# A cross-attention and ternary FFN kernel on one core: the context in one transfer, a silu of a constant column, a new instruction order

## The chip, the cores and the metric

The kernel runs on one core of a Trainium2 chip. The metric is the device time of one execution in microseconds (us), as the median of several runs. A core has a matmul engine (PE, with its weight loads shown apart as PEld), VectorE (DVE), ScalarE (ACT), GpSimd (POOL), and SyncE (SP), which here issues every transfer. Each engine works through its own instructions in program order; semaphores join them. Sixteen DMA engines carry out the transfers.

## The reference

For each of 8 batches there are 512 tokens of 512 features (x) and a context of 64 memory tokens of 512 features, with a mask. Cut to what matters:

```python
def linear_bit(x, w, g):                       # 8-bit activations, ternary weights
    x = g * x * rsqrt(mean(x*x) + 1e-8)
    s = 127 / clip(max|x|, 1e-4); xq = clip(round(x*s), -128, 127) / s
    m = mean|w|;  wq = round(tanh(w / (m + 1e-8))) * arctanh(m)
    return xq @ wq.T

n = layernorm(x)
a = softmax(where(mask, n @ ctx.T / sqrt(512), -1e30))
x = x + a @ ctx                                # zero where a batch's mask is all false
n = layernorm(x)
h = silu(linear_bit(n, w1, g1)) * linear_bit(n, w2, g2)    # 512 -> 2048
x = x + linear_bit(h, w3, g3)                  # 2048 -> 512
```

Each of w1, w2, w3 holds 2048 x 512 numbers in f32, 4 MB. The mean of |w| has to be known before a weight can be made ternary, so a whole weight passes through the chip before its first matmul.

## The kernel before, in words

**Tiles.** A batch is four tiles of 128 tokens, 32 tiles in all. For a tile, the work is a chain: layer norm and the scores (`pre`: statistics L560, the scaled tile `t` and its f16 parts `xh` L582 to 592, their transposes `xT`, the score matmuls `psc` L602, the masked scores `sc` L614 to 624), the exponentials (`expo`, L645, ScalarE), the softmax's scaling and the readout (`post`, L659 to 691: `ph`, its transpose `pT`, the matmuls `po` L683 from `ms`), the rms norm and 8-bit rounding of the FFN's input (`quantise_x`, L721 to 800: `xm`, the gain on POOL L736, the row maximum L741, the rounded `xm` L799/800, its transpose `zT`), the gate and up matmuls (L883, 16 groups of 8 matmuls per batch for each weight), silu (`gate`, L899, ScalarE), the product (L927, VectorE), its square (L932), the gain g3 (L940, POOL or VectorE), the maximum (L964), rounding (L997/999), a DMA transpose of the result (`hT`, L1002), and the down projection (`pd`, L825), which runs `LAG` = 3 tiles behind the gate.

**Weights.** Each weight comes in four pieces of 1 MB (`raw`, `load_w`). `measure_w` sums |w| of each piece on ScalarE (L353) or VectorE (L357) and joins the sums by a small matmul (`pm`, L363); `quantise_w` makes the pieces ternary (`tq`: tanh's threshold as a scaled rounding, L386 on POOL or VectorE, L387 on ScalarE), transposes them on PE (L396) and clips them into `w1T`, `w2T`, `w3T` (L390). The raw pieces, x of each batch and other large tiles share 9 buffers.

**The context.** `load_x(b)` loads, for an even batch, the contexts of two batches into one tile `both` (128 x 512, 256 KB, L473), from which `measure_mem` gets their scale; and for each batch the tile `mem`, which holds the same 64 rows twice, in partitions 0 to 63 and 64 to 127. It comes by two transfers of 128 KB (L478). `split_mem` makes two f16 parts of it (`ms`: the rounded part by L533 on ScalarE, the rest by L536 on VectorE), and transposes them to `mT` for the scores. `mem` has two buffers, `both` one.

**What sets the order.** The program first records every operation with its engine, a planner's cost in ns, what it reads and writes, and sometimes other engines that could do it. A planner that isn't part of the kernel has chosen an order and an engine for each; the result is the text `ORDER` (L151 to 190), decoded in `Plan.order`. Buffers are handed out in that order, and each engine gets its instructions in it. So the costs in the listing have no effect at run time, other than through the `ORDER` that was made with them. All loads, stores and DMA transposes are issued on SP's one queue, in that order. Before the change SP's order at the start is: mask, both_0, first half of mem_0, half of x_0, second half of mem_0, half of x_0, the four pieces of w1, g1, w2's first three pieces (two of them into space that w3T will take), g2, w2's last, x_1, both halves of mem_1, two pieces of w3, both_2, a piece, g3, x_2, the last piece, mem_2, both_4, the transpose mT_1, x_3, mem_3, and then the first transposes xT_1.

Of the kernel before, what the change touches and what calls it, by code (L numbers as in the profile page):

```python
# [41 lines left out]
AF = mybir.ActivationFunctionType  # L42
# [3 lines left out]
P = 128  # L46
# [13 lines left out]
PE, DVE, ACT, POOL, DMA = "PE", "DVE", "ACT", "POOL", "DMA"  # L60
DVE2 = "DVE2"
# [87 lines left out]


ORDER = """  # L151
c-jTQedKy+q5$yo@|^eQob#M>o^#G~UY3@Y?~m_~mM$$_y0o;kv@~?-($LV*(9*qHS{k~vG&D4{S3{SEhW==1XlUqOEnONKS{fQ!8d_R
f`lF@cem)c>QkVi1q!1OQa#WtmQU!`oMe2nrQ4#8uDpMg<p<+~=s!|CmNu{VXm7(g?h3-;Ux=r<{4%MJ;G^9VFn$&>8^oJCphZLbl)KB
QIs2bI$BlOqQXH=A4QFnSkPpCEZhMrOz>R;$BHKS(ikp3k-r{2;TdPnW47@egL)RZ03-%}GdPUq+oHKxy0p8h*^p%V0+dQewtLMQ1TsV
V)Wzo3^a#XxpWQ*?p;mIh3b7MT(a8N>j3L1RXw-=p{Roc*3AOvpr-1O0nuNmu9$^C!AWpXey_!mMb-PPqkprr%*Ubed_<Ev7~{=~pJkZ
0Ri1qA~lR+jN|%(;Yg&beSYW*c4M>a!i{E*)DzLip+}b(F-QR9=Ir51R3xy^M>s(HRc0m!@S4TnI7}X_L&$vWJ};b**!O4TA;z?K^#n&
&zKqaCG$R00DopWU?}$3-?42lWV&F)WWk#4vtKhgFl7ep$Kb$p_&!)MBQ^ozY>OX&HS-12VaM#JV8b@qEz@PMpv||~5m<vUn1LO$Wko^
aCZG(COj`I0GY1J42|qA@W0LF!U?Ihh#2x#0Ce3DqP|vVX$g(t>74FQF*@7IK6CTW-&9i_lu<r;vP-HL6ci_NEY>7RxW%k5Y*n%(xXZF
HY*(10}PjF=mTv0fI8(U-VY@L0uG4Nz7;2rJ^y22a&p8@13um?9#1!e9eA+E>)`2z0Xw*Ye~PzM99!oB4l0Dv?&aaB$PPbtPNK%A>_ge
wV45OPB<#X%6^5QuVft}HY_f;)3>xSmiEk{kv^Xo6pHRiVUPI09CH;#yo^7zrWBa#yL!i*f`2uFV~U92W%(?#k7<SN<rxfF<_|R$PbsB  # L160
}egRsliclL|=0UzQzxPE%$p)<N^O8oP-#^6}#LUdBeTRJ09{+zR!&XN<jQXXbL?J2zx#zr}-Oa^E>X&J(N(0^J_6KKe&z9<wHKhzo=^=
%lG&sAK~Xhf`4*Rekj)ksOI<-KjQLyLn!haf$&42z>m3=^eRq;_xKWj;?v?n_#I#8D`JK3^Plofe!_LcwKU>q!XNpiu#sv)34P8d<drb
yqvH2`SBwZV{wy@a8$ac5%8Qtk@5)p7nxFGnEs1~Q-wG*t!T(HH^G$T;FG5@dVp-hqq7s$P{FZ<4P#MVyk&-AeE{S4HxbR8wA&zAzUIi
jH#gsUa3sPK&sX3`7hT=_#t9RiS!c%-zcOp^$A^Z;?5!+}iHlz=Qw(ufVq;G_s&=J~VUTR86-3v)!DZNTn=_noLln|2+;#`V}C;292#J
!jok78Dwi0`N;aVi$XAH<nxh#gcxTdANH#f4;xWz<4dloQYLT`H<j-bqNgihmW~RjVSBKS%$k?xlxx7i;1ag>p@*i#HKSJuxEN(nr!vh
SCg0Wl`#jL>h=UIU)7rP(l)x=VDD>iVJZi-sOy(lp<0~p2~HpE;r=0e34U9T1v}TIG0y)QNqfvq>}WI`_hL}TPjPhN>(CrSzX9ixg&*2
Oxdaf={t!iznAAqMCnOcxuWLesM1ina#dX@Z8-{uQd7yxDWxFil(aID{#(i@9i=aK<gz@Kwn|r7$}?#o$F(M`$O&zyY~+?wmACR(+AD9
AfzpCE*oOt>Tlo%qN?tiAOXVqNbV^C<M`ZwCAW(Afr0mqVvX>J|Q7$U4@Tu%oQ7b8Z<y|=st4awbmG_i{`o8jO1;CnekSTbANv*E56{v
l#i116)hC>Cykz&B9V#6`?;7mEg2b{pH{+SZO3q;xzifRP@#Guqr<<ylDQKRZcIjC#ptfaK08iz4BR8ug8x>gz{;8jVf8TF!+VMZINSv
3QbFsDw{u^KUE))3aziB*B2mW5bLs|DD%(pnWpv<0leqgq$z*3|k4)?o)`wGo`c9=xhE*i@rhPMgDmwm?O=REc&{=h|0lRXeLoxPoJ?0  # L170
axnhYC|t-6Rn}H;Z5DZnYz&S@T9fWwR(UL?V_HwwmMgP>Jiqoi~iK^YF?{reU;M3`a^AMPnFVMwSoE#>{;K!7j0nuL7i&9)7n~7k7+<(
YfCMvU$lw7(^pzYn`wKitmX8LCh9NxN9tC4)puGJMGdI$^@85gUW~og(%;oO#zBjtiZ<1OwnSI`sLl1fo<LpgW38yCQ4OuoK>If%hYnT
-mGp!DiT0iz(`Wk8s-uTK)ZW*t`c-@CBdv=*GHzPWC>eGAu61;zxAh(x=rz5suTc`+^sY|yzJc`{%A<u2QNyg8OTDM}Q4!V5ve7_yv_Y
ThuLd%PsAAl8${6W2V}w?E+8CpOvC-?spY)-D(EuIwlO8hwI_o2YLIotEszFfPc%YOqb+&rK*rFY37zn9G(wG`!BWs4}N3=&X<AC0vjd
MnEb7kzDxr2>Y^f1;&!rU1f<ELor#L&;s-pQGw`80rWMa0OPWAlQbd9pG_28+hTpiE>goTr&JW=_tSm`(G0ls7&!n#RE(=2r$~wT*9#q
&YYC#?CC5cV}rFjlZCi@q_VK1DHkgYV6H|fh}y7%!3)4cOzmpEMmQwM>C6W#@ULRB`dVr=Bqh1TV~8mSUKD=KQ`lf*F2e@m<c_pr}VNF
v4Ax&o7T{}SShP&rOc5zvcAM2zFH5bgVScxD&mZp#}S;h($@c)bF*d*&4u-axiL$4ZPu-f)x~GCY%Z<5wJ@XB*4*HgRj^*H9$uOYe6xy
H%PQcDSv4zG*ID8|zM4;`V<qv;Y+Ds`Y^^Y~?xtvMth@Ca>lGtwh__b7{kipO?W_;no>RtA9JgxtVXmzz9^t+-z`wv-JjRs!u%h<U+Tj
WYZrpycpP0fDe!&2%7~vEy*$ErthF!K}IE@KD;HG`EYwi)Z>^QFD(3!Y<+`vh@iCcJWPw~*6;I<9yh%>{l_Qp=zqI<%3dyUUH?xbw!?%
gXE?Hj)1ihaQer(^#E*WIz*#!H8?M>eu!Hnyj3%X!D{+65ch8GGgy?TMYWR}ONg_80b-_Q3hhox8uW+m2^1?5#a?4$jdH?U56)tM<|9*  # L180
-N`_FWiAmIcNK1pWMEEv6t@2so5+0TN}GccW)o;tG#lg4safJ+DW;hbF>@o*-1KQH{)Df=s<#;g7fNp=5(B#({!)y8z<|eoR|~3H+SOX
owZYRpLWZ=IKOi9<m$9tL~`!U!Op+BEmCr_ZplrPo||{mE+)h&J7u@%v`N>!yK6T?D$c--xF0wnIg`3mAjIvvQTL5IAaC6w>9|9;;f&m
koAjE_kZj!xp~=pT5|8A)lvg4n@^A|t^2X%p=E#y1y$Z>a7lJ)NN?w`7T#>BF$Q!%Fi@Ph*AyxA4WJ79BjWo#AOSoIo@V+IX_h&Npnq=
i2$jpn7rZ*uiZ|!ZpDd~C@zvsP@wzu<sK{{TS{G3$%e<GiFSCS-s67hNjcqx+fY41kvMDmVg?xnq`_aG+%y|TCW1|IS&-i!AnLvP_tJn
Ub*S1;zxNZiYKDSzozy<dA9@8Hcz&O3Sw67gGp+CO=}^={tTi}?w!?p;0NXZ*MR!EgI_Z|mp$xZm*~-j5#b1Apvi{m@VNHNWfce9^!9M
<4n<KkDE7sh<c=e&5ggg&-Nc_!Ix^&-`*w@aKLpDEeRdU;7RJKm5JF@+-l+e$#*WpZfphm;Gum^3%c7uLWzL3NC&o*!Z&m1li#3Hv=)q
1tb^;Fff93&<Z9&JHSCScnNU03Fbj0Bw;5AgKiKBJ`VmEd=e~zT@VdlgJm!bQo%kL1?lh*<b&^nQt-Fn9^8UNI0%#BBcQ`)z=cv+4>I8
}Yy_h)8^UlJyo9+h7L3DkxC&4>3Ae%9Fdm$Od{_x*;WRu4^Dq`(f-qc!)vy*e!g|;YTVXuxhN-X}_QF4eg|Htk!(zAzOW`WqhU@SU?!t
X|3{T-X{D0au@s|
"""  # L190
BIG, XM, BOTH = 9, 2, 1
LAST = 1
# [6 lines left out]
def kernel(  # L199
# [62 lines left out]
    g_bc, g3_bc = fixed("g_bc", [P, 2, D]), fixed("g3_bc", [P, H])  # L262
# [116 lines left out]
    def quantise_w(i):  # L379
# [3 lines left out]
        for k in range(NK):  # L383
# [247 lines left out]
    def expo(*batches, tiles=range(NC)):  # L631
# [11 lines left out]
        def run():  # L643
# [500 lines left out]
```

## Time and profile before

| | |
|---|---|
| median of 3 runs | 428.87 us (427.7 to 428.94) |
| the profiled execution | 427.9 us, of which the span from first to last instruction is 425.8 us |
| mean granted clock of PE | 0.987 |
| PE busy | 388.8 us, 91% of the span |
| VectorE busy | 369.0 us, 87% |
| POOL busy | 368.7 us, 87% |
| ScalarE busy | 341.3 us, 80% |
| context loads | 16 of 128 KB, median 6.5 us from issue to landing |

Of the busy rows one reads which engine has no room left over the whole span; of the row of 40 slices (10.6 us each) where in time each engine is short of work. A group's line gives line number, engine, operation, the tile written and the tiles read, then busy time and idle time ahead of it with what released it. In the timeline, the first number is the start, the second the duration, and in brackets stand the idle time ahead and its releaser.

### The profile page before, as it was taken

The page shows a single profiled execution, that of the slowest core. Times are in us where ns is not written, and L with a number is a line of the kernel's source. Part 1 is how long each engine was busy: PE and PEld are TensorE (multiplying, and loading weights), DVE is VectorE, ACT ScalarE, POOL GpSimd, SP SyncE. Part 2 cuts the span into 40 slices and gives each one's busy share as a digit, 9 for nine tenths or more (in the row PEclk, how much of TensorE's full clock was granted, in tenths as well). Part 3 has the DMA queues.
Part 4 walks back from the last instruction along what each step waited for, and adds up shares of the span by engine and source line. Part 5 has one row for each costly group of instructions (what it writes and reads, how often), then busy time and mean ns, then how long its engine had stood idle before and what let it go on. Part 6 is the DMA issues. An engine that isn't in the chain of part 4 may idle for free.

```text
span 425.8 us, 6677 instructions
## 1 busy us (share of the span) xinstructions
PE 388.8 (91%) x2174; PEld 192.8 (45%) x2174; DVE 369.0 (87%) x832; ACT 341.3 (80%) x464; POOL 368.7 (87%) x330
## 2 busy tenths in 40 slices
PE   0563878999999999999999999999999999999996
PEld 0341534544444544454445444544454444444444
DVE  4689999999998998799989998999789888897772
ACT  1799999979899799598996898988686986774531
POOL 1789998998999999699999999999699979988650
PEclk9996899999999999999999999999999999999999
DMA  7999994497555578863589635864644546533272
GB/s 217 408 406 376 380 208 52 103 255 147 126 112 150 99 131 157 183 174 68 104 158 276 136 76 82 171 174 83 134 76 148 75 87 146 152 77 73 49 207 90
DMA packets 142514, 67.35 MB, mean 158 GB/s; under 512 B 133136, under 2 KB 133520, under 8 KB 140048
## 3 DMA queue, kind: packets, MB, share of 16 engines
q1 hardware_dynamic: 142480, 66.93, 63.4%
q8 instruction: 17, 0.28, 0.3%
q14 instruction: 17, 0.14, 0.1%
HBM read 25.76 MB, written 8.39 MB: 80 GB/s over the span
## 4 chain that ended last, share of the span: by engine, by line
PE 78%; DVE 6%; POOL 6%; DMA 3%; issue 3%; ACT 2%; SPq 0%; DVEq 0%; POOLq 0%; ACTq 0%
PE p L883 48%; PE pd L825 24%; PE po L683 3%; DMA zT<-xm 2%; PE psc L602 2%; POOL tq L386 2%; DVE st L560 1%; DMA both<-in_ctx_dram 1%; PE pd L854 1%; POOL t L586 1%; POOL xh L592 1%; POOL mv L291 1%; DVE zf L741 1%; DVE h L927 1%; ACT h L899 1%
## 5 line engine op out<-in xcount | busy, mean ns | idle before, releaser
L883 PEld LDWEIGHTS <-zT 128*128 128x128 f16 x1024 | 99.5, 98 | 122.0 <-issue 3.0
L940 POOL TENSOR_TENSOR h<-h,g_bc 128x1024 f32<-128x1024 f32 x55 | 130.4, 2377 | 2.7 <-ACT sq L932 2.1
L883 PE MATMUL p<-w1T,zT 128*128 128x512 f16 x512 | 120.4, 383 | 2.4 <-DVE zT L309 1.5
L883 PE MATMUL p<-w2T,zT 128*128 128x512 f16 x512 | 119.2, 379 | 1.1 <-DVE h L927 0.9
L825 PE MATMUL pd<-w3T,hT 128*128 128x512 f16 x496 | 117.8, 379 | 0.0
L927 DVE SCALAR_TENSOR_TENSOR h<-p,zf,h 128x1024 f32<-128x1024 f32 x64 | 81.9, 1280 | 14.9 <-PE p L883 8.4
L899 ACT ACTIVATE h<-p,zf 128x1024 f32<-128x1024 f32 x64 | 70.1, 1105 | 24.8 <-PE p L883 17.0
L932 ACT ACTIVATE sq<-h 128x1024 f16<-128x1024 f32 x64 | 67.2, 1050 | 17.0 <-DVE h L927 14.8
L825 PEld LDWEIGHTS <-hT 128*128 128x128 f16 x496 | 47.9, 98 | 55.6 <-DMA hT<-h 0.2
L964 DVE TENSOR_REDUCE hf<-h 128x1 f32<-128x2048 f32 x31 | 70.6, 2278 | 1.8 <-POOL h L940 1.7
L736 POOL TENSOR_TENSOR z<-xm,g_bc 128x1024 f32<-128x1024 f32 x29 | 69.8, 2423 | 1.4 <-ACT xm L725 0.6
L997 ACT ACTIVATE h<-h,hf 128x2048 f16<-128x2048 f32 x23 | 45.8, 1994 | 0.2 <-DVE hf L968 0.2
L741 DVE TENSOR_REDUCE zf<-z 128x2 f32<-128x1024 f32 x32 | 38.8, 1211 | 5.8 <-POOL z L736 5.7
L592 POOL TENSOR_TENSOR xh<-t,xh 128x512 f16<-128x512 f32 x32 | 37.3, 1168 | 2.0 <-DVE xh L591 1.2
L799 ACT ACTIVATE xm<-z,zf 128x512 f16<-128x512 f32 x42 | 28.1, 709 | 0.7 <-DVE zf L760 0.7
L731 ACT ACTIVATE xsq<-x,xf 128x512 f32<-128x512 f32 x32 | 22.9, 715 | 6.5 <-DVE x L691 6.0
L835 DVE SCALAR_TENSOR_TENSOR x<-pd,hf,x 128x512 f32<-128x512 f32 x31 | 23.1, 744 | 3.0 <-PE pd L825 2.6
L691 DVE SCALAR_TENSOR_TENSOR x<-po,mx,x 128x512 f32<-128x512 f32 x32 | 22.9, 745 | 1.3 <-PE po L683 1.2
L602 PE MATMUL psc<-mT,xT 128*128 128x128 f16 x256 | 19.7, 224 | 1.9 <-DMA xT<-xh 1.9
L560 DVE BATCH_NORM_STATS2 st<-x 128x6 f32<-128x512 f32 x32 | 21.3, 679 | 0.0
L602 PEld LDWEIGHTS <-xT 128*128 128x128 f16 x256 | 16.9, 101 | 8.5 <-DMA xT<-xh 3.5
L291 POOL TENSOR_TENSOR hf<-hf,neg_half 128x1 f32<-128x1 f32 x32 | 20.1, 634 | 0.2
(134 smaller groups left out, 483.4 us busy)
## 6 DMA issues: line engine op xcount, KB each, us to landing
raw<-in_L_ffn_w_dram SPq DMA_DIRECT2D x10, 1024.0 KB, 13.8
x<-in_x_dram SPq DMA_DIRECT2D x7, 1024.0 KB, 6.9
out_dram<-x SPq DMA_DIRECT2D x7, 1024.0 KB, 4.1
mem<-in_ctx_dram SPq DMA_DIRECT2D x16, 128.0 KB, 6.5
w3T<-in_L_ffn_w_dram SPq DMA_DIRECT2D x2, 1024.0 KB, 12.6
both<-in_ctx_dram SPq DMA_DIRECT2D x4, 256.0 KB, 8.2
x<-in_x_dram SPq DMA_DIRECT2D x2, 512.0 KB, 6.1
g_bc<-in_L_ffn_g_dram SPq DMA_DIRECT2D x1, 1024.0 KB, 14.9
```

The lines of the kernel that those rows point to most:

```text
L592: rest = lambda e, t=t, xh=xh: e.tensor_tensor(xh()[:, 1, :], t(), xh()[:, 0, :], ALU.subtract)
L602: T.matmul(psc()[:, c, :, :].rearrange("p s m -> p (s m)"), xT()[:, k, :], mT().rearrange("p (s d) m -> p d s m", s=2)[:, k % ND, :, :], s ...
L736: gain = lambda e, xm=xm, z=z: e.tensor_tensor(z(), xm().broadcast_to([P, 2, D]), g_bc(), ALU.mult)
L741: lambda i=i, z=z, am=am: V.tensor_reduce(am()[:, i, :], z(), AX.X, ALU.max, apply_absolute_value=True),
L825: T.matmul(po(), hT()[:, n * P : (n + 1) * P], w3T()[:, n, :], start=(n == 0), stop=(n == NH - 1),)
L883: T.matmul(ps()[:, k * HC : (k + 1) * HC], zT()[:, g * ND + d, :], weight(d, j * HW // HC + k), start=(d == 0), stop=(d == ND - 1),)
L899: lambda: A.activation(h()[:, j * HW : (j + 1) * HW], ps(), AF.Silu, scale=fac()[:, 0:1]),
L927: lambda: V.scalar_tensor_tensor(cols(), ps(), fac()[:, 1:2], cols(), ALU.mult, ALU.mult),
L932: lambda: A.activation(sq(), cols(), AF.Square, scale=(RMS / H) ** 0.5, accum_out=col(j)),
L940: run = lambda e: e.tensor_tensor(cols(), cols(), g3_bc()[:, j * HW : (j + 1) * HW], ALU.mult)
L964: lambda: V.tensor_reduce(col(2), h(), AX.X, ALU.max, apply_absolute_value=True),
L997: op(ACT, 1995, lambda: A.activation(hq(), h(), AF.Copy, scale=col(5)), [h], [(f, 5)], other=[(POOL, 1970, lambda: G.tensor_scalar(hq(), h ...
```

## The change

1. `load_x` loads `mem` with one transfer of 256 KB. Its source is the batch's 64 rows, broadcast to two copies; its destination the whole tile. As built, the source's access pattern is 2 copies with a stride of 0, 64 rows with a stride of 512 elements, 512 elements; the destination's is 128 partitions of 512.
2. A column `warm` of 128 numbers. Behind the exponential of batch 0's last tiles, ScalarE writes silu of a constant column to it. Nothing reads it. Silu's function table has to be loaded for it.
3. The planner's costs of four operations (a weight piece, the gains, the ternary rounding on VectorE, the context), and a new `ORDER`.

```diff
+    warm = fixed("warm", [P, 1])
...
-            op(DMA, (475, 650, 2750, 1400), lambda k=k: load(k), [raw[i, k]], [])
+            op(DMA, (475, 650, 2620, 1400), lambda k=k: load(k), [raw[i, k]], [])
...
-               other=[(POOL, 1970, lambda by=by: by(G)), (DVE2, 1700, lambda by=by: by(V))])
+               other=[(POOL, 1970, lambda by=by: by(G)), (DVE2, 1275, lambda by=by: by(V))])
...
-        for half in range(2):
-            op(DMA, (475, 650, 364, 500),
-               lambda half=half: Q.dma_start(mt()[half * M : (half + 1) * M, :], mem[b]),
-               [(mt, half)], [])
+
+        op(DMA, (475, 650, 700, 500),
+           lambda: Q.dma_start(mt(), mem[b : b + 1].broadcast_to([2, M, D])),
+           [(mt, 0), (mt, 1)], [])
...
         op(ACT, (204 + 53 * n) * len(batches), run, [(post_state[b][0], lo) for b in batches],
            [(att_state[b][4], lo) for b in batches], table="exp")
+        if batches == (0,) and hi == NC:
+            op(ACT, 220, lambda: A.activation(warm(), neg_half()[:, :1], AF.Silu), [warm],
+               [neg_half, *((post_state[0][0], at) for at in (0, lo))], table="silu")
...
-        op(DMA, (475, 650, 730, 800), lambda g=g, src=src: Q.dma_start(g_bc()[:, g, :], src.partition_broadcast(P)),
+        op(DMA, (475, 650, 1160, 800), lambda g=g, src=src: Q.dma_start(g_bc()[:, g, :], src.partition_broadcast(P)),
```

The new order on SP begins: both_0, half of x_0, mem_0, mask, half of x_0, the four pieces of w1, w2's first (into w3T's space), g2, two pieces, g1, w2's last, x_1, both_2, mem_1, a piece of w3, x_2, w3's other pieces, g3, both_4, mem_3, x_3, the transpose mT_1, mem_2, and then the first transposes xT_1. On PE the first transposed piece of w2 now stands ahead of the first gate's matmuls. Some operations have other engines: the gain L940 runs 49 times on POOL and 15 times on VectorE (55 and 9 before), L592 24 and 8 times (32 and 0), L736 25 and 7 times (29 and 3); one sum of |w| moved from ScalarE to VectorE. In ScalarE's order the silu of the constant stands directly ahead of the first silu L899.

More of the change, by code (lines that the diff above doesn't have):

```diff
@@ L151 @@
 ORDER = """
[L152 to L186, printed above, removed]
@@ L187 @@
-1tb^;Fff93&<Z9&JHSCScnNU03Fbj0Bw;5AgKiKBJ`VmEd=e~zT@VdlgJm!bQo%kL1?lh*<b&^nQt-Fn9^8UNI0%#BBcQ`)z=cv+4>I8
-}Yy_h)8^UlJyo9+h7L3DkxC&4>3Ae%9Fdm$Od{_x*;WRu4^Dq`(f-qc!)vy*e!g|;YTVXuxhN-X}_QF4eg|Htk!(zAzOW`WqhU@SU?!t
-X|3{T-X{D0au@s|
+c-jrt|L1b~f&lRM`TjoNzrD{n@AKu-rJ<#vp`oE!T^hPHG&J->Lk|sIx~rj~hc4}E=+e;A(9lCeLrY6TLqkJ%HLFWQmzIW>h8}wOJgcF
+hrOWQ?uXq6v204%g2;@N#L_i5>fCdmmK>@@-8N@*XBtZ()z=i05DrkWxq6^vpgC3ATA6$t#2!RF|fES<w0-zCdumA&M32ww!01;mUNKC
++#k_b$!KpJGg6a++w_yN2@{39`8njl5IAZ8#!q=`PU0a0Q?Wr!`9Q9CdqV#FR~iJ!m`<cK&iCQcwhyas1*1rl`u6CzLCz?66pGvW>aIV
@@ new lines @@
+T?AZv;&ihy?-3A|a6)NfU^~<TGMV?3sWB#D5cIqD9WBDzPLEghu^9oQMS#B5TBo$dGm7J@PrRA(qscXcB)Svm~NgM3`(7d9q7(h%Ip^F
+x4e`WP!|)3$jfHRF8;|MRLk)$Pg7JpOImz2h((${s-z4vcX2FDp{aEqk2@6u9GpUL+9ui*&v5hhibANGEVl%BAp;xbdrqG-;#McMP}&d
+RF>W`-;*n<PbIjI$uG&z=`QsLazgg#ugN|=pyE`8n38e&OL|3)s5P}FUyxfeK{crrJ*I~AnjX<px<zfMB)2D%)P>%W2XaPl=oI%2S)x<
+ak$kXQ`e$-WrKt?{n(V_douwY+FJzj_QGm-+G`FJ&>PA8pas}%5T#>qydpgUNr~^+^dx~LpbeZC*1NFqeBrDW`K2lXG&wNFms2cSSz2o
+n6ojOxdI>(gh2@RPe{X{3}3VoqY^o=ht5>sMw+?D<#tucKj&y|@Qy@WM7MW5*d^F&pcS7d~VG5^d(nF5EHDpRKi3})uE#KoB_6)*`V#1
@@ new lines @@
+y#(-R9n4j!cQ$atr!BX2#s8CH<g_%$@3RbEe6Z*$nfb0CQqmjHK?kGZSXp%$*1Ho~P*=bLAmjXC(T_XBmyIunPv!TXxA{+7$pBVSmf6m
+@XG^&zV5za~<X^?zuG^&}*j0T-pC+y3B)llO1q1Zo>|_BpYMn>=V;sUolr^!QI%q^gg?Q5}RZ~!kx{r8b`AsddNUF#Ud8T6)sG-*}H(*
+G#jB4Y>Elk8J}TqOoyFt8>Y%_nLNAX3T&AhGgY?7eZr2o5S(&|`-n}zI@@FCd=bvL&)EgvgkfRCykJZ0n45Eb_P~wVGmBwFIEg>A19rp
+$IRf`=RG6?CEr3(@7jD7k;f-^-BNv4iwg8uG72dhOu`9MKApXGigqRS6PwWNi?1SqIAr8P6l;DvKa|7WD<1ozE;1kqfhL3RHuyu&#s+Q
+sre3LtI4`I#*@~2#b!+eErz%<|F3Op^Jxiwei1OCFj#f9XuHh@!pE4=1v+6IRBEkEYNFauYx$nS(WmxU*O4TmrXv)V(dXgTe7a$277Nx
@@ new lines @@
+0<y3vOWw<~0WHAP~>|gD>&_!S%HF;D%fAN7&ac{9ee&B?yEQgisRRm&=eA+VBj2f+Ki?6*!kif+jrRn(sg)3^ay630(+zi62A2-{Az7g
+qkpgO+LcU;2fTXD6jExq0Aqoia?7ozAVJ~p)eB;LXIB`P{{HZq0YDYJTHkYp~k<%=j1?a@Cjie<Yg!xg+B^ovBekUg`DL7$~Qz!tP3dt
+i50OaOvK+R9bS{Vd`xT$1AZ<vgt%B0L*kHM2njJMG{vPj;-^Ad=m;&bB88QVuoCk^P5f7WDIBGa=!$ExAhe{E_!prnouodW7O%oo+=x#
+?QP_$|N=i2&EPgL%#COG;91)}9PP~XKIV)o6ec?&WiEXJUMwG1dnOG82(htH`dZE?Dve=QX;zk&VHEAfGrMx&2Z(>2bi#zG>Vpn9Op7?
+=qmwVDh3d>OXyZj{eB_PFBDEGyyBuO!KCQ9;Nnu~jJA%>(tipWKo)^8F}-jtvcmE%%OTFYrklcUNTQe2M75h<=5#e?{Pl#ue$Mjpr!Z7
@@ new lines @@
+kKyiQG47MN$e<LjFh^X%i`-bmXKwlrmC7>Y8<_Cs*Ww)RbaMSL(_Kc_bwjO(`f_Ijul_Dt#^Yl&SoMJW_UY-JD4!=_t>ovNV&2a$nghE
+2$)Bl&ah?&q`VDnPcT7@07KaQbuw~ohTdWEDy|@e36@SSKZ4OrKmh91Er*VpwyI^f|RR*6;0hMWi?P1>UUC4ZOI=i@2EFL(!ZCQ=E7{t
+JN2#%m8nwG=ZdB;l!~%avPz(hwUk;>m+EVIq7Bux(pQmMm(yxo+bDJADnFN#>Rt_L-z!xmuQZgE8r9lLM*Wj=Qe#>|D`<87OSPlq)#v&
+_=_*-uY1Xx(R#02Y%1rBLwWwxvte%vxc2rvGR4W>3tzi6<T2q^9Q-3IRHK~=fgL=?DQ`=fY%jzAqpf|OVdemrjtRlUkexqUisOI#EI#q
+$XRy*28ZE0=&p%(S6de`#$NxP{3qh7R#-qBOqRgI#SKDSGHR|8t0$Bl2)U)2xPkbYO^YG0?diLPtEY6~qey826Pt|9HDPwj^mGM3s(!&
@@ new lines @@
++3|Y6JbM_w1OSFrKuXcF_YB=t-kv?6tEV*00*yJQ*>>YjHiHca59g(}7Xer+V19>oYy6&yBP3oxallpbzz>Ue(jaw|dIB8-06bul0?-F
+rM_iE^9?IrRzq<c<2jzV2|{Jo;DxG(s*VJ?X?EXo?#hpBW$$Hjae~P##mn)88d+ncG<WXRikavX3e0DkXka2dc>$AfSN{Fg+^d*w6Ga6
+w`L0E%$6Y=G&<TbqisaYs4+Ar#+N8+er@E<ojEYlXli7QFN}f-&9}^iIWnhcXhc-Wtf85aG{<Jv{86u(L-bc;WYmqCy)`;!+1%+n<85<
+<_QuqFZk+5VqlJDl^M+>rVno#ts+cz;i85$!rp&YbDMIEL&CINmGa$m|!O&0+9gTl8+o*wLbTm7tZlBC7YS_@4n`d*05W1L>HAC3SIV<
+!V^dXv~2@0&Vb+La&c?Y8=%2);G4OFy3)&fP)-nyAZ^x7<0pF0z4hwf(CDxeE`hJanMdZ>$jG52U{Jt58NqXX(W5$lW|<_5jCv(_4YjE
@@ new lines @@
+?APW1F_Wa4INlZBf+<Y-Ek>mUXb&)^|?Xu37I`SJbhR*4Um|H<YsOXz4WViruw()(h)_Zg$IF+EJ@-jjgu5a$;88%2_KLSOcqW6|A*=w
+nkRoDmwpZjht_-f%BtvwC?uOT00F3+8b+Ug`9;&TTSbgwX&Y9loPQxcG%fESL<%wtf;No8%MUs&d{maZ`sJcI&u4Cb?umwuqSrNE;(WQ
+U1w{T@t^IT^RS{0a1wZD-<-W&cHVX(xZ<SkckPs&b|Ov`XY7QtcdAa!xjR`q<5X}H*PVi$#1DJoG@Pb$a6)d&N#Ua1c3ODmZ1BYa_}?9
+f(|GP2oh`oMl1)2p44sFQv%_u&C)_(eIc+zNlkQ9Bfoc5YjBv*(;4JRB$dR2QCfpcKxe}gW>|}7-t>O|MyBhAeMYr$%26yqqo#L{a^$-
+r>k~_vVobv+bLtA%pxZ?Kk%>5A0a2<b-8~A{Cc<#RZ|7z{=1+VZYZpb_0g&W2Z_ciY0j9Yc*_*3_a8!qok?#*4gL+s+L+jQ^l33uI=J8
@@ L190 @@
+(y?=7v4Xow{qBci(bXZqyyR$cwvWZ|&yXh_`VUxZpnAiWl<+xa#FS>>6I(qrJWRqq}ow9`<(LC*INvyugimbMI&O;3oZ}yYenB@Oob0L
+oek&xqC0;zjQ<X+n(elyrY-&vi|S9g7+_8#9w<2?;|hm{n;ydIlt?jyoI;%n%>rn`e(20^}T`D_lI80zq-GAUwN;*u{ZJK{==Jk9Y5m%
+|L#rwXFl!g{=w_|cmG2l`A^=%FZ&gL;>~?JsQPt(;Me@CH}rXb;fMXE9|T|dOCJU;KjEkSzxZum3JU(t4+RH*??(bHXa+C+SN_pI`9;6
+sw}RJxH0b$b9|f`C>bHY<F!OJIC&2#N|9y}MBtIMUgIq8Ox<N6>2fbhz6oQRk4xR;DzZO)2QBVy)Fb?X$B)~x<2nWj`8LWa-Fb&edI@k
+oWU>+=j{{u5->jV
 """
```

## The prediction

> **What bounds the kernel now.** I read three views, in this order: the engines' busy times, the table of 10 us stretches, and the timeline rows around the waits of the first 85 us.
>
> ```profile
> PE 388.8 (91%) x2174; PEld 192.8 (45%) x2174; DVE 369.0 (87%) x832; ACT 341.3 (80%) x464; POOL 368.7 (87%) x330
> ...
> PE   0563878999999999999999999999999999999996
> ...
> GB/s 217 408 406 376 380 208 52 103 255 147 126 112 150 99 131 157 183 174 68 104 158 276 136 76 82 171 174 83 134 76 148 75 87 146 152 77 73 49 207 90
> ...
> raw<-in_L_ffn_w_dram SPq DMA_DIRECT2D x10, 1024.0 KB, 13.8
> ...
> mem<-in_ctx_dram SPq DMA_DIRECT2D x16, 128.0 KB, 6.5
> ```
>
> The matmul engine is busy for 388.8 of 425.8 us, so it idles for 37.0. The row of slices says where: from the eighth slice to the last but one every digit is 9. Idle time lies in the head, and 3.6 us in the tail. The stretches give the sizes (columns: elapsed, PE, PEld, DVE, ACT, POOL, granted clock, DMA share, GB/s):
>
> ```profile
> 20.00:30.00 10.00, 5.98 (x82) 4.74 (x83) 8.01 (x32) 8.96 (x14) 8.07 (x10) 1.00 1.05 401
> 30.00:40.00 10.00, 3.99 (x37) 2.66 (x35) 9.45 (x27) 9.24 (x18) 9.42 (x12) 0.81 1.03 374
> 40.00:50.00 10.00, 6.85 (x53) 4.13 (x51) 9.54 (x22) 9.10 (x9) 9.56 (x12) 0.68 1.02 427
> 50.00:60.00 10.00, 8.53 (x72) 4.99 (x71) 9.87 (x27) 10.00 (x15) 9.30 (x13) 1.00 1.19 243
> 60.00:70.00 10.00, 8.30 (x67) 4.95 (x68) 9.48 (x30) 9.34 (x12) 8.44 (x11) 1.00 0.69 118
> 70.00:80.00 10.00, 8.19 (x79) 5.11 (x77) 10.00 (x21) 9.76 (x14) 9.15 (x8) 1.00 0.15 29
> 80.00:90.00 10.00, 10.00 (x48) 4.55 (x47) 9.45 (x33) 8.61 (x12) 9.38 (x12) 1.00 0.88 220
> ```
>
> All eight stretches up to 80 us together hold 32.3 us of PE idle time; from 82.94 us (the first down projection) only 1.1 us follow before the tail. So the time is the moment at which PE becomes continuously busy, plus work that is the same in both kernels (4325 PE instructions in each). Three limits act on that moment: the one DMA queue, which moves 374 to 427 GB/s from about 4 to 58 us and is full; then VectorE and ScalarE at 95 to 100%; and single waits between them. These are the rows at which the changed kernel will meet them:
>
> ```profile
> 8.53 1.28 ACT L533 ACT_TABLE_LOAD   x1 [8.53 <-DMA mem<-in_ctx_dram]
> 37.58 0.71 ACT L533 ACTIVATE ms<-mem,mf 128x512 f16<-128x512 f32 x1
> 38.20 0.72 ACT L799 ACTIVATE xm<-z,zf 128x512 f16<-128x512 f32 x1
> 41.78 1.03 PE L883 MATMUL p<-w1T,zT 128*128 128x512 f16 x2 [1.46 <-DVE zT L309]
> 47.53 1.28 ACT L899 ACT_TABLE_LOAD   x1
> 61.59 0.62 PE L602 MATMUL psc<-mT,xT 128*128 128x128 f16 x8 [1.09 <-DMA xT<-xh]
> 82.94 1.25 PE L825 MATMUL pd<-w3T,hT 128*128 128x512 f16 x5
> ```
>
> The first shows that the first context is already waited for; the second, that batch 1's context is scaled on ScalarE (L533) just ahead of the L799 that makes the first gate's input; the sixth, that batch 1's scores wait for a DMA transpose (xT), which goes through the same queue as every load.
>
> The sums below are made against the profiled execution, 427.9 us (span 425.8 and 2.1 around it). It stands 1.0 under the median of 428.87; the three runs lie between 427.7 and 428.94.
>
> **The context in one transfer.** Removed: 8 issues on SP (16 transfers become 8). SP's issue takes about 0.47 us (465 to 474 ns in the rows of L478) and SP isn't the bound while the queue is full: worth nothing as long as transfers are queued behind it, which they are until 58 us. Bytes: the same, 256 KB a batch. What changes is the shape. Today each half is 64 rows of 2 KB. The new source pattern, as built, is 2 copies with stride 0, then 64 rows, then 512 elements, so its outermost dimension has two entries; every transfer in the trace has 64 or more there. No row shows a transfer like it, so I bound it.
> - Lower end: it spreads over the 16 engines like the rest. 256 KB at the queue's 407 GB/s is 0.64 us, what the two halves take now; cost 0.
> - Upper end: it is cut in two along the outermost dimension, each copy on one engine. 407 / 16 = 25.4 GB/s an engine, so 128 KB take 5.15 us, against 0.64 us for a spread share. While the queue is full, the two engines fall behind the others by 4.5 us with each load, if they are the same two each time. Every other transfer has a piece on them too and lands when its last piece does.
>
> I take the upper end: a transfer has to be cut along some dimension to be shared out, the outermost is the nearest, and it is the one in which this pattern differs from every row shown (2 against 64 or more). A gain from fewer transfers is excluded in the full stretch, since bytes set the pace there.
>
> The Trainium skill, "DMA: Bandwidth & Descriptors", section "Rules for kernel authors", speaks against this edit in as many words: a leading zero-stride broadcast of c copies confines the whole DMA to at most c engines; its section "Why a DMA increments its semaphore by 16 and not by 1" adds that these are the lowest-numbered ones, hence the same two each time. By that rule the sum is the upper end below; by the rows alone (the halves land spread, at the queue's pace) it would be nothing.
>
> **The upper end walked through the new queue order** (landing on the two slow engines; 1 MB is 2.6 us, from the raw loads that land at 12.40, 15.01, 17.57, 20.10 now).
> 1. Batch 0's context is third in the queue and lands at about 12.1 instead of 8.44. The first ScalarE scaling (L533) waits for it. The last w1 piece lands at 24.6 instead of 20.10; the mean and the first ternary rounding (now 24.89) move by 3 to 4 us.
> 2. Then w3T, g2, two pieces, g1, one piece, x_1 and both_2: 24.6 + 5 x 2.6 + 3 x 0.65 = 39.6, and mem_1 at about 45. ScalarE's scaling of it still stands directly ahead of the L799 that feeds the first gate. Today that gate starts 4.2 us after the scaling (37.58 to 41.78): about 49 instead of 41.78, +7. Queued behind the waiting ScalarE instruction: two ternary roundings of w2 (L387), a |w| sum and the first silu.
> 3. Then raw_2_0, x_2, three pieces and g3 (6 x 2.6), both_4 (0.65): 61.3; mem_3 66.4; x_3 69.0; mT_1 and mem_2, about 75.6; then xT_1_1, on which batch 1's first scores and, in PE's program order, the second tile's gate wait. New: mem_2 and mem_3 both stand ahead of that transpose. With some 2 us for the transposes the scores start at about 77.6 instead of 61.59: +16.
> 4. PE idles 3.5 us between 60 and 80 now; part of that goes, since VectorE can clip weights and copy zT ahead while PE waits. So PE becomes continuously busy 12.5 to 16 us later; I take 14.
> 5. Loads of batches 4 to 7 come while the queue is half empty (29 to 276 GB/s by slice). Each can hold back the hT or zT transpose behind it by up to 5 us; L825 of a tile runs three tiles late, which covers most: 0 to 5 us in all, I take 0 to 1.
>
> **The silu of a constant.** It adds one 128 x 1 activation, about 0.2 us by the nearest row (the accumulator read, 0.19), and moves the silu table load (1.28 us) ahead of it. The number of table loads stays 16. In the new order the pair still stands directly ahead of the first L899, behind the L799 of tile 1, so the load is no earlier on ScalarE than at 47.53 now. A gain up to 1.28 would need idle ScalarE time ahead of the first gate's end, and ScalarE is 91% busy in 40 to 50; a loss is at most 0.2. I take 0. In the upper end the wait for mem_1 covers it in any case.
>
> **The new order.** Counts at the ends: POOL loses about 20 us of work in all (L940 55 to 49, L592 32 to 24, L736 29 to 25), VectorE gains about 12 (L940 9 to 15, L592 0 to 8), ScalarE about 7. If the loads did spread, following the new order with the rows' durations puts the first ternary rounding at 24.05 (24.89 now), the first gate at 41.6, w3's mean at 58.5 (60.05) and the first L927 at 61.5 (63.53): PE saturates 2 us earlier, the sum -2. It can also lose: VectorE rises from about 93% to 96% between 90 and 316 us, and each of its operations that runs beside POOL stretches (L536 took 0.75 and 1.67 us): 0 to 3 us. In the upper end these 2 us are already in the walk.
>
> **Sum.** 427.9 + 14 + 0.5 for step 5 = 442.4; I say 442.5.
>
> **The rivals.**
> - *The transfer spreads, and the order shows its gain*: 427.9 - 2 = 426, or 427 from the median. For it: a broadcast over 128 rows (g, 256 KB) lands in the queue's pace, so stride 0 by itself doesn't hurt. Against: that one has 128 rows outermost. It decides if mem_1 lands before about 38 us. It is the case on the other side.
> - *It spreads, and the fuller VectorE stalls PE in the steady part*: 427.9 - 2 + 5 = 431. For it: 96%; against: PE's backlog of three tiles.
> - *Two pieces, but not the same engines each time, or the lag is caught up between loads*: then one lag of 4.5 and one own transfer, some 5 to 8 us instead of 14: 433 to 436.
> - *The steps add up without any slack*: 16 + 5, 449 to 451.
>
> **How the numbers follow.** Two pieces with the lag summed: 0.70 (own range 436 to 451); two pieces partly hidden, 0.12; spread with gain, 0.10; spread and neither, 0.04; spread with stalls, 0.04. A measurement of this kernel tells about 0.3%, 1.3 us, from no change. Faster: 0.10; same: 0.05; slower: 0.85. The range goes from 428, which leaves out most of the spread case, to 452, above the bound of the last rival.
>
> **What would show it.** The context's row in the list of DMA issues: 8 of 256 KB with a median far above 6.5 us even in quiet stretches (there at least 5, today 2.7). ScalarE's L533 waiting for mem twice, for about 3.5 and some 4 us; the first L883 near 49; the scores of batch 1 near 78 with xT named as the releaser; the DMA share in 30 to 70 us lower, because fourteen engines run out of work while two go on. Against me: a median near 5 to 6.5 with the DMA share at 1.0 through 50 us. I would be wrong in size if the order has slack that I didn't see in step 3, above all if mem_2 or mem_3 are issued after the transpose in time.

## The result, and the profile after

The changed kernel takes 456.73 us as the median of 4 runs (456.23 to 457.49), against 428.88 us before. The ratio is 1.0658, with a 95% interval of 1.0633 to 1.0683: 27.9 us slower, above the forecast's 442.5 us and 4.7 us above the upper end of its range.

Busy times, slices and the list of DMA issues on the page of the changed kernel:

```profile
PE 394.5 (87%) x2174; PEld 196.3 (43%) x2174; DVE 381.9 (84%) x786; ACT 346.5 (76%) x474; POOL 350.1 (77%) x343
...
PE   0273570999979999998999899999999999999996
...
GB/s 215 368 392 256 382 141 79 142 107 155 143 106 96 169 115 94 144 164 179 47 128 222 168 104 73 130 70 213 127 78 127 98 104 100 180 65 94 92 138 117
...
mem<-in_ctx_dram SPq DMA_DIRECT2D x8, 256.0 KB
```

PE is busy 5.7 us longer in a span that is 29.3 us longer (455.1), so most of the loss is PE idle time. The row of slices shows two kinds: in the head, a 0 in the seventh slice, where the kernel before had an 8; and, new, single slices of 7 and 8 far behind the head. The context's row has lost its last number: its issue-to-landing time, the reading that the prediction had named, isn't given. (Two other rows of the page, x in two transfers of 512 KB and the 1 MB of g3, have lost theirs too.)

The stretches of the head, in the same columns as before:

```profile
30.00:40.00 10.00, 5.68 (x73) 4.00 (x70) 9.81 (x29) 10.00 (x16) 9.77 (x8) 1.00 0.76 273
40.00:50.00 10.00, 0.59 (x2) 0.50 (x2) 5.01 (x16) 3.79 (x10) 7.76 (x8) 0.53 1.02 339
50.00:60.00 10.00, 7.50 (x71) 5.74 (x72) 8.76 (x20) 9.97 (x11) 6.24 (x10) 0.79 0.72 296
60.00:70.00 10.00, 7.85 (x63) 4.59 (x59) 8.57 (x27) 10.00 (x15) 9.24 (x12) 1.00 1.10 153
70.00:80.00 10.00, 0.27 (x3) 0.18 (x4) 6.70 (x21) 1.40 (x3) 3.33 (x5) 0.56 1.09 92
80.00:90.00 10.00, 10.00 (x66) 5.78 (x65) 3.42 (x3) 9.50 (x11) 6.19 (x6) 0.75 0.60 107
```

From 40 to 50 and from 70 to 80 us PE nearly stands still (0.59 and 0.27 us busy), ScalarE mostly (3.79 and 1.40); VectorE and POOL have work for a part of the time. The timeline has the waits that answer to the rows shown of the kernel before:

```profile
13.74 1.28 ACT L534 ACT_TABLE_LOAD   x1 [13.74 <-DMA mem<-in_ctx_dram]
48.77 0.72 ACT L534 ACTIVATE ms<-mem,mf 128x512 f16<-128x512 f32 x1 [6.21 <-DMA mem<-in_ctx_dram]
52.70 2.63 PE L887 MATMUL p<-w1T,zT 128*128 128x512 f16 x8
79.83 1.03 PE L603 MATMUL psc<-mT,xT 128*128 128x128 f16 x8 [9.73 <-DMA xT<-xh]
101.10 1.03 PE L829 MATMUL pd<-w3T,hT 128*128 128x512 f16 x4
```

Batch 0's context is there at 13.74 us instead of 8.53; batch 1's at 48.77, where ScalarE stood idle for it for 6.21 us; the first gate starts at 52.70 instead of 41.78, the first scores of batch 1 at 79.83 instead of 61.59, the first down projection at 101.10 instead of 82.94. So 18.2 us are lost by then. The rest, 354.0 us instead of 342.9, is lost behind it. In the head's part of the chain of waits (start, length, what) the two longest links are transfers:

```profile
29.27 19.48 DMA mem<-in_ctx_dram
...
65.70 14.09 DMA xT<-xh
```

The later loss is seen at batch 5's context in the timeline of the changed kernel (the rows of PE and of SP's queue, others left out):

```profile
121.34 0.55 SPq L479 DMA_DIRECT2D mem<-in_ctx_dram  x1
122.00 4.45 SPq L299 DMA_TRANSPOSE zT<-xm  x1
...
130.85 1.90 PE L887 MATMUL p<-w2T,zT 128*128 128x512 f16 x8 [2.58 <-DMA zT<-xm]
```

The transpose behind the load holds SP for 4.45 us (some 1.25 us in quiet places, as at 118.70) and lands late, and PE waits 2.58 us for it. This happens while the DMA engines together move few bytes (122 GB/s from 120 to 140 us).

### The profile page after: what moved, and what is told of

The parts are those of the page before. It is cut to its first block, busy times and chain, and to the rows that moved or that the text cites. A ratio compares the mean times of both kernels' runs of the same rounds, so it can differ in the third digit from the quotient of the medians.

```text
span 455.1 us, 6674 instructions
## 1 busy us (share of the span) xinstructions
PE 394.5 (87%) x2174; PEld 196.3 (43%) x2174; DVE 381.9 (84%) x786; ACT 346.5 (76%) x474; POOL 350.1 (77%) x343
## 4 chain that ended last, share of the span: by engine, by line
PE 63%; DMA 15%; ACT 5%; POOL 5%; DVE 4%; issue 3%; SPq 0%; POOLq 0%; ACTq 0%; DVEq 0%
PE p L887 38%; PE pd L829 20%; DMA xT<-xh 6%; DMA mem<-in_ctx_dram 4%; DMA zT<-xm 3%; PE po L687 2%; PE psc L603 2%; POOL z L740 2%; DMA hT<-h 1%; DVE h L931 1%; ACT h L903 1%; POOL xh L593 1%; ACT w2T L354 1%; PE pd L858 1%; DVE w3T L391 1%
## 5 line engine op out<-in xcount | busy, mean ns | idle before, releaser
L887 PE MATMUL p<-w1T,zT 128*128 128x512 f16 x512 | 123.5, 389 | 1.2 <-DMA zT<-xm 0.5
L944 POOL TENSOR_TENSOR h<-h,g_bc 128x1024 f32<-128x1024 f32 x49 | 117.7, 2409 | 8.9 <-ACT sq L936 8.8
L829 PE MATMUL pd<-w3T,hT 128*128 128x512 f16 x496 | 119.9, 382 | 0.0
L740 POOL TENSOR_TENSOR z<-xm,g_bc 128x1024 f32<-128x1024 f32 x25 | 62.0, 2486 | 14.9 <-ACT xm L729 12.4
L603 PE MATMUL psc<-mT,xT 128*128 128x128 f16 x256 | 20.8, 233 | 16.2 <-DMA xT<-xh 14.1
L593 POOL TENSOR_TENSOR xh<-t,xh 128x512 f16<-128x512 f32 x24 | 27.8, 1161 | 8.1 <-ACT xh L591 7.9
L803 ACT ACTIVATE xm<-z,zf 128x512 f16<-128x512 f32 x45 | 30.8, 711 | 1.3 <-POOL zf L764 0.7
L603 PEld LDWEIGHTS <-xT 128*128 128x128 f16 x256 | 18.0, 105 | 23.5 <-DMA xT<-xh 15.1
L591 ACT CAST xh<-t 128x512 f16<-128x512 f32 x31 | 18.6, 607 | 9.2 <-DMA xT<-xh 8.6
```

Source lines behind the costliest of these rows:

```text
L593: rest = lambda e, t=t, xh=xh: e.tensor_tensor(xh()[:, 1, :], t(), xh()[:, 0, :], ALU.subtract)
L603: T.matmul(psc()[:, c, :, :].rearrange("p s m -> p (s m)"), xT()[:, k, :], mT().rearrange("p (s d) m -> p d s m", s=2)[:, k % ND, :, :], s ...
L740: gain = lambda e, xm=xm, z=z: e.tensor_tensor(z(), xm().broadcast_to([P, 2, D]), g_bc(), ALU.mult)
L829: T.matmul(po(), hT()[:, n * P : (n + 1) * P], w3T()[:, n, :], start=(n == 0), stop=(n == NH - 1),)
L887: T.matmul(ps()[:, k * HC : (k + 1) * HC], zT()[:, g * ND + d, :], weight(d, j * HW // HC + k), start=(d == 0), stop=(d == ND - 1),)
L944: run = lambda e: e.tensor_tensor(cols(), cols(), g3_bc()[:, j * HW : (j + 1) * HW], ALU.mult)
```

## The experiments

The theory to be tested: the broadcast source is carried by two engines, each later piece on these two waits, and that is the whole loss (A). Its rivals: the new order loses by itself (B); or a stride of 0, or one transfer in the place of two, is what hurts, whatever its outermost dimension (C).

**The changed kernel with two halves.**

```diff
-           lambda: Q.dma_start(mt(), mem[b : b + 1].broadcast_to([2, M, D])),
+           lambda: [Q.dma_start(mt()[h * M : (h + 1) * M, :], mem[b]) for h in range(2)],
```

> The changed kernel with each context loaded in two halves again; its order, the constant's silu and everything else stay. Theory A (the broadcast transfer is carried by two engines, and their lag is the whole loss): the 27.9 us come back and the order's own gain shows, about 427 us, first down projection at about 81 us (82.94 before, 101.10 in the changed kernel). Theory B (the new order itself loses, by stalls of PE or by mem_2 and mem_3 standing ahead of the transposes): well above 428.9, some 435 to 450 us, with PE waiting for xT or zT as in the changed kernel.

428.5 us; ratio to before 0.9983 (0.9958 to 1.0007). The loss is gone, so B falls. The rows that answer to those above, from its timeline:

```profile
38.81 0.72 ACT L534 ACTIVATE ms<-mem,mf 128x512 f16<-128x512 f32 x1 [2.20 <-DMA mem<-in_ctx_dram]
...
43.37 2.16 PE L887 MATMUL p<-w1T,zT 128*128 128x512 f16 x8
...
61.94 1.03 PE L603 MATMUL psc<-mT,xT 128*128 128x128 f16 x8 [1.81 <-DMA xT<-xh]
...
83.57 1.03 PE L829 MATMUL pd<-w3T,hT 128*128 128x512 f16 x4
```

The gain of 2 us that I expected of the order didn't come. In the new queue order mem_1 stands behind both_2, and even spread over all engines it comes 2.20 us too late for ScalarE; the first gate is at 43.37, not at 41.6. (In four traces with the head's contexts spread, ScalarE scales batch 1's context at 38.5 to 39.1 us, 37.58 before, and the first gate starts at 43.1 to 43.9, 41.78 before. That this alone takes the gain isn't shown.)

**The kernel before with the one transfer.** In the first of its two issues the whole context is loaded, the second issues nothing:

```diff
-               lambda half=half: Q.dma_start(mt()[half * M : (half + 1) * M, :], mem[b]),
+               lambda half=half: half or Q.dma_start(mt(), mem[b : b + 1].broadcast_to([2, M, D])),
```

> The kernel before with one edit: where the first half of a context was issued, the whole is loaded by one broadcast transfer, and the second issue is gone. Order as before. Theory A: the two engines lag by some 4.5 to 7 us with each load; in this order mem_2 stands ahead of the first xT transpose as well and mem_3 behind x_3 too, so the loss is about the same, 445 to 457 us. Theory B: the transfer costs nothing by itself, about 429 us.

463.62 us, ratio 1.0799 (1.0754 to 1.0843): more than expected by A's upper figure. The transfer loses in the old order too, and more there (some 34 us) than in the new one (28). By the first down projection, at 99.43 us, 16.5 us are lost; the rest is lost behind it. Its waits of PE behind 110 us:

```profile
PE p L883 <- DMA zT<-xm: 4.9, 1, 4.9
PE psc L602 <- DMA xT<-xh: 4.9, 1, 4.9
PE pd L825 <- DMA hT<-h: 4.6, 2, 2.8
```

They are 14.4 us, where the changed kernel has 7.8 us behind 101 us and the kernel before 1.1 us behind 84 us.

**How many copies.** The source is cut to fewer rows and broadcast to more copies; the bytes written stay 256 KB in one transfer.

```diff
-           lambda: Q.dma_start(mt(), mem[b : b + 1].broadcast_to([2, M, D])),
+           lambda: Q.dma_start(mt(), mem[b : b + 1, : P // 16].broadcast_to([16, P // 16, D])),
```

> The changed kernel, but the one transfer takes only the first 8 of the 64 context rows and broadcasts them to 16 copies (leaves out 56 rows of each context, so the attention is over other numbers; work and bytes written are the same, 256 KB in 128 rows of 2 KB). The source's outermost dimension is 16, still with a stride of 0. Theory A: a sixteenth on each engine, no lag: about 427 us, as with the halves. Theory C (a stride of 0, or one transfer instead of two, is what hurts): stays near 456 us.

With 4 copies (`P // 4`, `[4, P // 4, D]`):

> As the run with 16 copies, but 32 of the rows in 4 copies (32 rows left out). Theory A: four engines with 64 KB each, 2.6 us at the queue's pace per engine instead of 5.15, a lag of 1.9 us per load instead of 4.5, so about 0.4 of the loss: 434 to 440 us. Theory C: near 456 us.

And, run later, with 8:

> The changed kernel with 16 of the 64 context rows in 8 copies (48 rows left out of the computation). Eight engines with 32 KB each: 1.3 us instead of 0.64. With 16, 4 and 2 copies the times were 428.3, 437.4 and 456.7; the extra time of an engine over a spread share is in the ratio 0 : 1.9 : 4.5 us a load, and 0.64 for 8 copies, so by the same line 430.5 to 432 us.

| copies (outermost dimension) | KB on each engine, if one copy goes to each | time, us | ratio to before |
|---|---|---|---|
| 16 | 16 | 428.26 | 0.9978 (0.9963 to 0.9992) |
| 8 | 32 | 432.24 | 1.0075 (1.0044 to 1.0105) |
| 4 | 64 | 437.35 | 1.0180 (1.0152 to 1.0209) |
| 2 (the change) | 128 | 456.73 | 1.0658 (1.0633 to 1.0683) |

C falls: with 16 copies it is one transfer, with a stride of 0, and nothing is lost; nor is anything gained over two halves (428.26 and 428.5). The loss follows the number of copies. The run with 8 lay just above its expectation, the one with 4 within it. The row of the context in the list of DMA issues with 16 copies:

```profile
mem<-in_ctx_dram SPq DMA_DIRECT2D x8, 256.0 KB, 6.8
```

The last number is there with 16 copies and missing with 8, 4 and 2.

The packet records of the traces show the number of engines directly. A context is 128 packets of 2 KB. For the contexts behind 90 us, where little else passes, the changed kernel has two of them under way at a time; with 4 copies it is four, with 8 copies eight, with 16 copies or halves up to sixteen (some overlap by a few ns where one ends and the next starts). The time from a context's first packet to the end of its last is 5.2 to 6.6 us with 2 copies, 3.0 to 3.9 with 4, 1.9 to 3.0 with 8, and 1.1 to 2.0 with 16.

They also show, in one place, that it is the same two engines. In the changed kernel's trace only two streams of 8 KB packets run from 57.4 to 62.3 us; the other fourteen engines are through with what was queued. Batch 3's context had been issued at 48.77 us. It doesn't start on the idle engines, but at 62.985 us, 2 ns after the last packet of the one stream, and at 63.751 us, 2 ns after the last packet of the other. So it had to wait for the two engines that batch 1's context had put behind.

**Head and steady part.** The broadcast for batches 0 to 3 alone, halves for the rest (`if b < 4 else`), and the opposite:

> The changed kernel, with the broadcast transfer only for the contexts of batches 0 to 3, which are all loaded by 66 us; batches 4 to 7 in halves. If the part of the loss after the first down projection (354.0 us from there to the end, 342.9 before) comes from the loads of batches 4 to 7, this run keeps the 18 us of the head and loses the rest: 446 to 449 us. If it is an after-effect of the late head (other phase of the engines, a lower clock), it stays at about 456 us.

> The opposite: halves for batches 0 to 3, the broadcast transfer for 4 to 7. By the first theory 428.5 + 10 = 437 to 440 us, with PE waiting for xT and zT transposes behind each of those loads; by the second about 428.5 us. By the step in the prediction (the three tiles between gate and down projection cover these waits): 428 to 430 us.

447.83 us (ratio 1.0441, 1.0408 to 1.0474) and 438.45 us (1.0205, 1.0143 to 1.0267), in both cases against 429.30. The first four loads cost 18.5 us, the last four 9.2 (6.1 to 11.5 by the interval); together 27.7, the 27.9 of the change. So the loss behind the head isn't an after-effect of the late head. PE's waits behind 102 us, first with the broadcast for the first four (as long in all, 2.0 us, as with halves throughout), then for the last four:

```profile
PE p L888 <- ACT h L904: 1.3, 2, 0.9
PE p L888 <- DMA zT<-xm: 0.4, 1, 0.4
PE pd L830 <- DMA hT<-h: 0.3, 1, 0.3
```

```profile
PE psc L604 <- DMA xT<-xh: 5.0, 2, 3.0
PE p L888 <- DMA zT<-xm: 2.6, 2, 2.3
PE p L888 <- ACT h L904: 1.7, 1, 1.7
PE pd L830 <- DMA hT<-h: 0.4, 1, 0.4
```

The 7.6 us for xT and zT are the larger part of the 9.2. PE hardly waits for the down projection's input (0.4). The score or gate matmuls that wait stand ahead of it in PE's program order; when PE gets to it, its input is there.

**The loads of the head one by one.** The broadcast for batch 0 alone, batch 1 alone, batches 2 and 3 (`if b == 0 else`, and so on):

> The changed kernel with the broadcast transfer for batch 0 alone, the other seven contexts in halves. In the changed kernel batch 0's context landed at 13.74 us instead of 8.44. If each load costs its own lag and nothing is given back: 4.5 to 5.5 us over the run with the halves (428.5), 433 to 434. If VectorE and ScalarE catch it up, as the prediction assumed for a part: 429 to 432.

> The same for batch 1 alone. Its packets took about 124 ns each beside the 8 KB packets of w3 in the changed kernel, against 84 ns in quiet stretches: if that sets the lag, 64 x 0.124 = 7.9 less the 0.6 of a spread share, so 5 to 7.5 us: 433.5 to 436. If the lag is 4.5 as in the prediction's step: 433; if part of it is covered: 429 to 432.

> The same for batches 2 and 3. Both stand in the queue ahead of the transpose that batch 1's first score waits for. If the four loads of the head add up to the 18.5 us of the run with the first four: what batches 0 and 1 leave, 7 to 9 us: 435.5 to 437.5. If they only bind because the first two loads had put the two engines behind, less: 429 to 433.

| broadcast for | time, us | ratio to before | first score of batch 1, us |
|---|---|---|---|
| none (halves) | 428.5 | 0.9983 (0.9958 to 1.0007) | 61.94 |
| batch 0 | 435.22 | 1.0161 (1.0133 to 1.0189) | 68.04 |
| batch 1 | 433.62 | 1.0127 (1.0092 to 1.0162) | 65.47 |
| batches 2 and 3 | 436.45 | 1.0189 (1.0165 to 1.0212) | 67.74 |
| batches 0 to 3 | 447.83 | 1.0441 (1.0408 to 1.0474) | 79.82 |

Taken singly, none of the loads is free, and nothing shows that a part is given back: over the halves, the ratios add 1.8, 1.4 and 2.1%, in sum 5.3%, and the four together 4.6%, a difference within the intervals. Batch 1 came at the lower edge of what its packets gave (433.5 to 436), batches 2 and 3 within theirs. Batch 0's load cost more than I expected (435.2 against 433 to 434), because I had counted its lag from the old order. ScalarE's first work, which waits for this context, starts at 6.21 us with halves in the same order and at 13.52 in this run: the load comes 7.3 us later, not 4.5 to 5.5, and the score is 6.1 us late.

The load is that slow because packets are slow on all engines while it passes. From 8.5 to 12.5 us the changed kernel's 2 KB packets take 122 ns at the median, against 84 ns in the run with halves. The DMA share is the same, but far fewer bytes move (the changed kernel, then the run with halves; the last two numbers are DMA share and GB/s):

```profile
8.50:12.50 4.00, 0.00 (x0) 0.00 (x0) 0.00 (x0) 0.00 (x0) 0.00 (x0) 1.00 1.05 286
```

```profile
8.50:12.50 4.00, 1.60 (x17) 1.02 (x15) 3.93 (x10) 2.20 (x3) 2.17 (x3) 1.00 1.05 400
```

The same happens at batch 1's context: from 42 to 47.9 us the 8 KB packets of the loads behind it take 451 ns, and 313 ns once it is through. What makes them slow stays open. It isn't the size of the neighbours' packets: batch 0's context ran beside 2 KB packets, and batch 3's took about 84 ns a packet beside 8 KB packets from 63 to 65 us.

**mem_2 and mem_3 behind the transposes.** In the decoded order, the two loads are moved to behind batch 1's four xT transposes; the broadcast stays. (The lines that note the operations' numbers in `mark` are left out here.)

```diff
         codes = array("H", zlib.decompress(base64.b85decode("".join(ORDER.split()))))
+        late = [self.mark["mem_2"], self.mark["mem_3"]]
+        rest = [c for c in codes if c >> 2 not in late]
+        at = 1 + max(i for i, c in enumerate(rest) if c >> 2 in [self.mark[f"x_1_{k}"] for k in range(4)])
+        codes = rest[:at] + [c for c in codes if c >> 2 in late] + rest[at:]
```

> The changed kernel, with mem_2 and mem_3 moved in the queue to behind batch 1's four xT transposes; nothing else. If two of the four lags stand ahead of the first score of batch 1, it starts some 8 to 10 us earlier than at 79.83 (first gate at 52.7 as it was, then the 18.6 us that lie between gate and score with the halves: 71.3), the first down projection at about 92 instead of 101.1, and the time is 446 to 451 us. If it is the first two loads alone, or issue slots held by other waits, nothing moves: 455 to 458 us.

456.88 us, ratio 1.0642 (1.0579 to 1.0705): nothing gained, a miss. But not for the reason given for that case. Its timeline:

```profile
70.37 0.62 PE L610 MATMUL psc<-mT,xT 128*128 128x128 f16 x8 [0.17 <-DMA xT<-xh]
...
97.36 1.89 PE L836 MATMUL pd<-w3T,hT 128*128 128x512 f16 x4 [6.52 <-DMA hT<-h]
```

The score starts at 70.37, as worked out (71.3), 9.5 us sooner. Then the two lags meet the next thing in the queue that PE needs, the transpose hT of the first down projection: 6.52 us of waiting, and SP's issue of that transpose took 6.95 us. The lead at the down projection is 3.7 us (97.36 against 101.10), and from there to the end this run takes 358.9 us against 354.0. So moving these loads didn't place the lag out of the way; it came down on what was next in the queue.

**The constant's silu, earlier.** The run with halves, with the silu of the constant moved to directly behind the last exponential of batch 0 (the line that notes its number in `warm` and the edit to halves are left out here):

```diff
         codes = array("H", zlib.decompress(base64.b85decode("".join(ORDER.split()))))
+        rest = [c for c in codes if c >> 2 != self.warm]
+        at = 1 + max(i for i, c in enumerate(rest) if c >> 2 in self.ops[self.warm].deps)
+        codes = rest[:at] + [c for c in codes if c >> 2 == self.warm] + rest[at:]
```

> The run with the halves, with the constant's silu moved in ScalarE's order to directly behind batch 0's last exponential, so that silu's table is loaded some 30 us ahead of the first gate. If the 1.28 us ahead of the first silu were on the path: 427 to 428 us, up to 1.3 us less than the run with the halves (428.5). If ScalarE only swaps the place of a load in a stretch where it is full: no difference beyond 0.3%, 427.5 to 429.5 us.

428.84 us, ratio 0.9992 (0.9964 to 1.0020). The table load stands at 27.51 us in this run, and at 47.06 in the run with halves, directly ahead of the first silu:

```profile
27.51 1.28 ACT L655 ACT_TABLE_LOAD   x1
```

Nothing that can be told from the halves alone: the silu's early place is worth nothing here. A run without the constant's silu wasn't made; together with the new order it is worth no more than the 0.4% that the interval of the run with halves allows.

## Why the prediction was right or wrong

- **Two pieces on two engines, the upper end:** right, and shown, by the number of copies above. The Trainium skill, "DMA: Bandwidth & Descriptors", section "Rules for kernel authors", says that a leading broadcast of c copies confines the transfer to at most c engines; the times with 16, 8, 4 and 2 copies agree (428.26, 432.24, 437.35, 456.73 us). The packet records show two streams, and batch 3's context waiting for the two that batch 1's had put behind; they don't name the engines.
- **What one load takes, 5.15 us, lag 4.5:** about right in quiet stretches, too small in the full one. In the packet records the four contexts behind 100 us take 5.2 to 6.6 us each (1.5 to 3.1 us before, in halves, behind 90 us), with a median of 84 ns a packet: 64 x 84 ns = 5.4 us. But batch 1's packets took 124 ns each: 64 x 124 ns = 7.9 us, and batch 0's context came 7.3 us later than in halves. In both places the packets of all engines were slow, as shown above; why stays open. I had priced the load by the mean pace of the queue. The trace of before had a row: its packets of batch 1's context took a median of 115 ns.
- **Steps 1 to 3, the walk:** right in kind. Batch 0's context at 13.74 (said: 12.1), batch 1's at 48.77 (45), the first gate at 52.70 (49), the score at 79.83 (77.6), with the releasers named. The differences of 1.6 to 3.8 us go with the load that was priced too low.
- **Step 4, a part given back by VectorE and ScalarE working ahead (14 of 16):** wrong. From the score to the first down projection it took 21.3 us, as before (61.59 to 82.94). Nothing that was done ahead shortened it: in the stretch from 70 to 80 us VectorE was busy 6.70 and ScalarE 1.40 us, and 8.6 us of ScalarE's idle time ended with the same transpose xT. The head lost 18.2 us, 18.5 by the run with the first four.
- **Step 5, the later loads (0 to 5, taken as 0 to 1):** the step that failed. They cost 9.2 us, where the sum had 0.5. I had let the down projection's three tiles cover them. But PE works through its order, and it was the score and the gate of the next batch, ahead of the down projection in that order, that waited for xT and zT. Nothing is covered by work that stands behind the waiting instruction. I had set the upper bound at one lag for all, where each of four loads has a transpose behind it.
- **The sum, 442.4:** it is 14.3 us short. The later loads are 8.7 of them (9.2 against 0.5), the head 4.2 (18.2 against 14), and 1.0 is the profiled execution that the sum started from, which lay under its median; 0.4 is left over.
- **The new order, -2:** wrong in its size. With the transfer spread the changed kernel is at most about 0.2% faster (0.9983 with halves, whose interval holds 1; 0.9978 with 16 copies). Batch 1's context, moved behind both_2, is waited for there, which fits, but no run isolates it. The rival "the transfer spreads, and the order shows its gain" had its price too high.
- **The silu of the constant, 0:** agrees with the run that moved it, whose interval holds 1; no run left it out.
- **Readings of the kernel before:** SP's issue of a half context took 0.47 us only at the median up to 60 us, the longest 2.68. The view shows VectorE at 91% from 90 to 316 us, not 93, and at 93% in the new order with halves, not 96. The 4325 PE instructions stand in no view; the pages show 2174 matmuls and as many weight loads in both kernels. None of these moves the sum.
- **What would show it:** the landing time of the context's row, named as the first sign, wasn't given. ScalarE's two waits for the context came (5.2 us longer than before and 6.21 us; said were about 3.5 and some 4), and the scores waited for xT. The DMA share, said to be lower from 30 to 70 us, was lower in two of four stretches (0.76 against 1.03 from 30 to 40 us, 0.72 against 1.19 from 50 to 60), equal in one (1.02) and higher in one (1.10 against 0.69).

## What to carry to other kernels

Before a load is folded into one broadcast, look at the outermost dimension of its access pattern: at 2 it cost 28 us in a kernel of 429, at 16 nothing, and the single transfer was worth nothing over two halves in any case. Price such a lag by each transfer behind it that an engine needs next, and let nothing cover it that stands behind the waiting instruction in an engine's order. Price packets by the rows of their own stretch, not by the queue's mean: here the same 2 KB took 84 or 122 ns.

## What the runs showed of the hardware that I had not expected

- The lag of a few engines reaches the others through the issue: SP's issue of the load behind batch 1's context took 6.97 us, and the engines together moved less meanwhile (273 GB/s at a share of 0.76 from 30 to 40 us, 374 at 1.03 before). SP's row in the changed kernel's timeline, of the piece of w3 behind mem_1:

```profile
30.85 6.97 SPq L327 DMA_DIRECT2D raw<-in_L_ffn_w_dram  x1
```

- While batch 0's context passes over two engines, the packets of all sixteen are slow: 286 GB/s at a share of 1.05, against 400 GB/s with halves (8.5 to 12.5 us, shown with the loads of the head).
- A long wait of PE costs more than itself. In the stretches in which PE stood, 40 to 50 and 70 to 80 us, the granted clock was 0.53 and 0.56, and the first group of eight matmuls behind the score at 79.83 took 3.62 us; later groups took 1.89. The mean granted clock of the changed kernel is 0.962, of the one before 0.987.
